# Moving weight means, first shared products and a feed-forward block in a one-core decoder kernel

## The chip, the cores and the metric

The kernel runs on one core of a Trainium2 chip. Five engines work side by side, each with its own in-order queue: TensorE (PE, with PEld for its weight loads), VectorE (DVE), ScalarE (ACT), GpSimd (POOL) and SyncE (SP, which issues the DMAs here). [...] The metric is the time of one execution in microseconds (us) on the device. A profile is one such execution, recorded instruction by instruction; its span runs from the first to the last instruction.

## What is computed

One decoder layer on 16 sequences of 256 tokens with 512 features, in float32:

```python
x = _layernorm(x + mamba(x))            # 2 x + out projection inside
x = _layernorm(x + long_convolution(x, ctx, ctx))
x = _layernorm(x + ffn(x))
```

The first block normalises x, projects it to gate z, inner xi, states B and C and step dt, runs a 4-tap convolution and a state recurrence, and projects back. The second, for each of 32 heads h (8 positions of the 256 each) and along the 512 features:

```python
kv = v[:, :, :, None, :] * x2[:, :, None, :, :]     # 8 x 8 products
y  = irfft(rfft(kv, n) * rfft(k, n), n)[..., :L] + kv * skip
out = einsum('bhijl,bhil->bhjl', y, x1)
```

Here x1 = x2 = ctx. The third is a linear layer with weight W, plus the two best of eight low-rank experts, chosen by a gate.

## The kernel before

**First stage** (to about 757 us): eight groups of 512 tokens. In each, a hand-written list `order` of ten products, counted by i = 0 to 9: ("x", p), ("z", p), ("b", 0), ("c", 1). For each i the program issues `first_products` on TensorE, `finish_products` of the product before, `first_sums` of this one and `finish_sums` of the one before (VectorE and ScalarE). `head_means(0)` and `head_means(1)` (tile `xm`, line 598) come at i = 6 and 8; `yps` at i = 9 (line 679). After the list, `spread_heads` (line 740) spreads a small result over two `mm` banks and two `wh` tiles, and `gated` (line 754) multiplies them into the gates on VectorE. The tiles xm, yps, mw, wh and d_lg take turns in the two PSUM buffers of `ps_t`; a tile waits until the readers of the tile two before it are done.

Three functions prepare the feed-forward weights w_f (128 x 4 x 512) and the gate weights w_gl (128 x 4 x 136), so that the layer norm in front of that block costs nothing later. `with_identity` (line 512) adds the residual to w_f. `chunk_sum` (523) adds the four chunks on GpSimd. `centred` (534) multiplies the sum with a constant matrix on TensorE (tile mw) and subtracts the result from each chunk in four VectorE instructions (540). All three run in group 1: with_identity at i = 2, chunk_sum at i = 3 and 4, centred at i = 5 and 6.

**Second stage** (from about 757 us): 32 heads, each in two parts q = 0 and 1 of eight sequences. The convolution is a product with Toeplitz blocks T. Its result y is four PSUM banks in two pairs: the first holds the output blocks 1 and 0, the second 2 and 3. `convolve` (1018) computes full 128 x 128 blocks (1027) and then quadrants of 64 x 64 (1042). Two products that the blocks 2 and 3 share are formed once: `seeded` (1008) multiplies the Toeplitz block T with xs, a sum on GpSimd (997), into bank 3, and `spread_seed` (1014) copies it by halves on ScalarE, with the halves exchanged, into bank 2 (1016). The convolution adds to both. In the first part of head 0 there is no seed (`late`): the quadrants come first, then six full blocks in the order `FIRST`.

VectorE multiplies each pair of y with the context (`multiplied`, 1077), reduces it (`reduced`, 1087) and prepares the next head's kv (`products`, 156). The new y of the next part takes the same banks, so its first writer into a pair waits for `multiplied` of that pair.

The feed-forward block of head h - 1 runs inside head h: gate products (1190), and four blocks of `feed_forward` (1223) into the tile `base`, for k = 0 to 3, two matmul instructions each. Block 0 stands ahead of the seed of part 1, blocks 1 and 2 behind it, and block 3 at the start of the next head, ahead of `turned_gates` (1213), the seed of part 0 and `lora` (1219). The tile base has one PSUM buffer; heads 0 and the start of head 1 don't use it. `gates` (1115 to 1142) and `store` (1158) go to VectorE and ScalarE.

The order on each engine is that of the program: no scheduler changes it.

Of the kernel before, what the change touches and what calls it, by code (L numbers as in the profile page):

```python
# [8 lines left out]
F32 = mybir.dt.float32  # L9
# [5 lines left out]
P = 128  # L15
B, S, D = 16, 256, 512
# [12 lines left out]
NH = 8  # L29
# [14 lines left out]
SHARED_AT, DIAGONAL_AT = 3, 5  # L44
NT, NC = 6, 6
FIRST = ((1, 0), (2, 0), (2, 1), (3, 0), (3, 1), (3, 2))

QUADRANTS = (
    (0, 0, 1), (1, 0, 1), (2, 0, 1), (3, 0, 1),
# [22 lines left out]
def decoder_kernel(  # L72
# [108 lines left out]
    with ExitStack() as s1:  # L181
# [370 lines left out]
        for g in range(groups):  # L552
# [97 lines left out]
            for i, (kind, p) in enumerate(order):  # L650
                if g == 1 and i == 2:
                    with_identity(w_f)
                if g == 1 and i in (3, 4):
                    w, cols = ((w_f, D), (w_gl, NG))[i - 3]
                    total = chunk_sum(w, cols)
                if g == 1 and i in (5, 6):
                    centred(*sums.pop(0))
                if g == 1 and i in (3, 4):
                    sums.append((w, cols, total))
                if i == 6:  # L660
                    ms = [head_means(0)]
                if g == 0 and i == 0:
                    al, be = first_products(
                        kinds[kind], p, True, None,
                        lambda: begun.append(begin_products(w_xi, order[1][1], False)),
                    )
                else:
                    al, be = first_products(
                        kinds[kind], p, i % 3 == 0, begun.pop(0) if begun else None
                    )  # L670
                if i == 8:
                    ms.append(head_means(1))
                if i == 9:


                    yps = ps_t.tile([P, S], F32, tag="tr", name="yps")
                    for ht in range(HT):
                        for b in range(GB):
                            nc.tensor.matmul(
                                yps[b * HP : (b + 1) * HP],  # L680
                                sel[:, ht].rearrange("p q h -> p (q h)"),
                                Bs[ht][:, b * S : (b + 1) * S],
                                start=(ht == 0),
                                stop=(ht == HT - 1),
                            )
                if before is not None:
                    finish_products()
                to = places(kind, p)
                u = first_sums(al, be, to)
                if i == 8:  # L690
                    states(1, stepped(ms[1], spreads[2]), spreads[3])
                if i == 6:
                    ms = [stepped(ms[0], spreads[0])]
                    spreads.append(spread(1, 1))
                if g == 0:
                    if i == 1:
                        parts = decays()
                    if i == 2:
                        nc.scalar.activation(A, A, AF.Exp)
                        nc.vector.tensor_scalar(A, A, -1.0, None, ALU.mult)  # L700
                    if i in (1, 2, 4):
                        next(parts)
                if i == 9:
                    yT = q3.tile([P, S], F32, tag="vn", name="yT", bufs=1)
                    nc.scalar.copy(yT, yps)
                if before is not None:
                    finish_sums((lambda: next(parts)) if g == 0 and i == 2 else None)
                if g == 0 and i == 3:
                    next(parts)
                if g == 0 and i in later:  # L710
                    for n, (w, k) in enumerate(later[i]):
                        ins = weight_sums(nc.gpsimd, w, k)
                        if n == 0:
                            wait_for(ins, mixes[-1])
                if i == 7:
                    states(0, ms[0], spreads[1])
                if i == 8:
                    outputs(0)
                    outputs(1)
                    if more:  # L720
                        rt = to_dram(rms(xs_next))
                    if g == 0:
                        behind = []
                        w_sums = w_o_sums(behind)
                        next(w_sums)
                before = (kind, p, al, be, u, to)
                if i < 2 and late:
                    normalised(g - 1, late.pop(0))
                if i == 1 and more:
                    xs_next = load_x(g + 1)  # L730
# [186 lines left out]
    with ExitStack() as s2:  # L917
# [87 lines left out]

            return xs, Td, pair_sum, differences

        def seeded(y, T, xs, q):

            nc.tensor.matmul(bank_of(y, 3), T[:, SHARED_AT, :], xs[:, q], start=True, stop=True)  # L1012

        def spread_seed(y):
            for a, b in ((0, HP), (HP, 0)):
                nc.scalar.copy(bank_of(y, 2)[b : b + HP], bank_of(y, 3)[a : a + HP])  # L1016

        def convolve(y, kv, T, Td, q, between=None, late=False, early=None, ahead=None):

            begun = set() if late else {2, 3}

            def full(lb, mb, w):
                nc.tensor.matmul(  # L1027
                    bank_of(y, lb),
                    w,
                    moving(kv, q, mb),  # L1030
                    start=not late and lb not in begun,
                    stop=False,
                    skip_group_check=True,
                )
                begun.add(lb)

            def quadrant(lb, a, b):
                r, c = a ^ (lb in SWAPPED_IN), b ^ (lb in SWAPPED_OUT)
                start = lb not in begun and (lb, c) not in begun
                begun.add((lb, c))  # L1040
                rows, cols = [slice(i * HP, (i + 1) * HP) for i in (r, c)]
                return nc.tensor.matmul(  # L1042
                    bank_of(y, lb)[cols],
                    T[rows, DIAGONAL_AT, (b - a) * HP : (b - a + 1) * HP],
                    moving(kv, q, lb)[rows],
                    start=start,
                    stop=False,
                    skip_group_check=True,
                )

            if not late:
                full(1, 0, T[:, FULL_AT[1, 0], :])
                full(3, 2, T[:, FULL_AT[3, 2], :])
                full(3, 0, Td[:, 1, :])
                full(2, 1, Td[:, 0, :])
            begin = [quadrant(*e) for e in QUADRANTS[:4]]
            one = p2.tile([P, 1], F32, tag="one", name="one")
            seen = nc.scalar.copy(one, nhalf[:, 0:1])
            for ins in begin:
                wait_for(seen, ins)  # L1060
            for e in QUADRANTS[4:8]:
                quadrant(*e)
            for e in QUADRANTS[8:]:
                wait_for(quadrant(*e), seen)
            if late:
                for n, (lb, mb) in enumerate(FIRST):
                    if n == 0 and ahead is not None:
                        ahead()
                    if n == 1 and early is not None:
                        early()  # L1070
                    if n == 3 and between is not None:
                        between()
                    full(lb, mb, T[:, FULL_AT[lb, mb], :])
# [154 lines left out]
        for h in range(HX):  # L1228
# [8 lines left out]
            if h:  # L1237
# [5 lines left out]
                        cTs.append(load_c(h + 2))  # L1243
                if rest is not None:
                    base, o_r, xa = rest
                    feed_forward(base, o_r, (3,))
                    turned = turned_gates(xa)
                seeded(y, T, xs, 0)
                spread_seed(y)
                if rest is not None:  # L1250
                    lora(base, [turned])
            if ff:
# [14 lines left out]
                if ff:  # L1267
                    folded()
            red = p2.tile([P, NQ, NL, BQ * NH], F32, tag="red", name="red")
            convolve(y, kv, T, Td, 0, late=h == 0, ahead=ahead)  # L1270
            if h == 0:
                v_after = vT_ahead[0]
            ws = skip_sum(sk_next)
# [10 lines left out]
            else:  # L1284

                prs = []
                for i in range(2):
                    prs.append(multiplied(y, cT, 0, i))
                    behind = products(v_n, cT_n, kv_n, 0, (i * NL // 2,), kept)
                for i, pr in enumerate(prs):  # L1290
                    reduced(pr, red, 0, i)
            y = new_y()

# [8 lines left out]
                base = ps_b.tile([P, D], F32, tag="base", name="base")  # L1302
                feed_forward(base, o_l, (0,), True)
            if nxt:
                seeded(y, T, xs, 1)
            if ff:
                feed_forward(base, o_l, (1, 2) if nxt else (1, 2, 3))
            if ready is not None:
                store(*ready)
            if nxt:  # L1310
                spread_seed(y)
            if nxt:
                products(v_n, cT_n, kv_n, 1)
                more_next = prepared(kv_n, T_n)
# [168 lines left out]
```

## Time and profile before

| what | value |
| --- | --- |
| median of 3 runs | 1433.55 us (1432.08 to 1434.61) |
| the profiled execution | 1433.9 us |
| its span | 1432.1 us |
| TensorE busy | 1414.5 us |
| VectorE busy | 1210.5 us |
| GpSimd busy | 492.3 us |
| ScalarE busy | 414.5 us |
| mean granted TensorE clock | 0.997 |

In lists of waits each line names who waited, for whom, the total in us, how often and the longest. A line of a timeline has the start, the length in us, the engine, the line of the kernel, the operation, output and inputs, the shape and how many instructions were merged; in brackets the idle time of the engine before it and who ended it. A float32 matmul shows as two instructions. Neighbouring TensorE instructions overlap in the record[...]: 512 columns start 0.43 us apart and last 0.59. A granted clock of 1.0 is TensorE's full speed.

### The profile page before, as it was taken

The page shows a single profiled execution, that of the slowest core. Times are in us where ns is not written, and L with a number is a line of the kernel's source. Part 1 is how long each engine was busy: PE and PEld are TensorE (multiplying, and loading weights), DVE is VectorE, ACT ScalarE, POOL GpSimd, SP SyncE. Part 2 cuts the span into 40 slices and gives each one's busy share as a digit, 9 for nine tenths or more (in the row PEclk, how much of TensorE's full clock was granted, in tenths as well). Part 3 has the DMA queues.
Part 4 walks back from the last instruction along what each step waited for, and adds up shares of the span by engine and source line. Part 5 has one row for each costly group of instructions (what it writes and reads, how often), then busy time and mean ns, then how long its engine had stood idle before and what let it go on. Part 6 is the DMA issues. An engine that isn't in the chain of part 4 may idle for free.

```text
span 1432.1 us, 18826 instructions
## 1 busy us (share of the span) xinstructions
PE 1414.5 (99%) x6882; PEld 908.0 (63%) x6882; DVE 1210.5 (85%) x2133; ACT 414.5 (29%) x900; POOL 492.3 (34%) x662
## 2 busy tenths in 40 slices
PE   9999999999999999999999999999999999999997
PEld 7887788787888888888884444444444444444443
DVE  6978778877888787887847999999999999999996
ACT  3423323233232332322301323222322232222221
POOL 5451010100100201002005565556555655565562
PEclk9999999999999999999999999999999999999999
DMA  8013021120121201212002212221222122112200
GB/s 299 33 39 130 14 76 46 38 83 8 58 68 40 79 13 39 83 44 84 15 26 96 66 45 73 67 73 45 75 66 65 54 74 67 60 59 67 73 26 23
DMA packets 49165, 89.16 MB, mean 62 GB/s; under 512 B 8880, under 2 KB 13360, under 8 KB 49072
## 3 DMA queue, kind: packets, MB, share of 16 engines
q1 hardware_dynamic: 49072, 87.96, 19.2%
q8 instruction: 54, 0.88, 0.3%
q14 instruction: 39, 0.32, 0.1%
HBM read 70.62 MB, written 17.32 MB: 61 GB/s over the span
## 4 chain that ended last, share of the span: by engine, by line
PE 87%; DVE 2%; issue 1%; POOL 1%; ACT 0%; POOLq 0%; DVEq 0%
PE mm L329 16%; PE y L1027 15%; PE y L1042 12%; PE s L329 11%; PE base L1223 8%; PE s L783 5%; PE mm L783 5%; PE y L1012 4%; PE gl L1190 2%; PE base L1219 2%; PE tr L146 1%; PE xm L598 1%; PE mm L740 1%; PE mm L874 1%; PE s L874 1%
## 5 line engine op out<-in xcount | busy, mean ns | idle before, releaser
L1077 DVE TENSOR_TENSOR pr<-y,cT 128x1024 f32<-128x1024 f32 x126 | 148.1, 1217 | 47.1 <-PE y L1042 47.1
L1042 PE MATMUL y<-kv 64*64 64x512 f32 x1536 | 179.6, 598 | 0.0
L587 DVE SCALAR_TENSOR_TENSOR acc<-xi,wc,acc 128x512 f32<-128x512 f32 x192 | 141.9, 753 | 7.4 <-ACT acc L583 1.7
L1087 DVE TENSOR_REDUCE red<-pr 128x128 f32<-128x1024 f32 x126 | 147.1, 1208 | 0.0
L156 DVE TENSOR_TENSOR kv<-tr,cT 128x1024 f32<-128x1024 f32 x124 | 145.4, 1213 | 0.0
L1027 PE MATMUL y<-kv 128*128 128x512 f32 x272 | 128.2, 594 | 0.6 <-ACT y L1016 0.4
L1042 PEld LDWEIGHTS y<-kv 64*64 64x64 f32 x1536 | 52.2, 132 | 119.0 <-issue 96.7
L1223 PE MATMUL base<-w_f,ol 128*128 128x512 f32 x248 | 124.0, 603 | 0.0
L1027 PE MATMUL y<-kv,Td 128*128 128x512 f32 x248 | 116.5, 592 | 0.0
L67 POOL TENSOR_TENSOR rs_a<-ve_a,nhalf 128x1 f32<-128x1 f32 x32 | 19.0, 594 | 243.0 <-DVE ve_a L65 243.0
L1256 POOL TENSOR_TENSOR ol<-o,red 128x512 f32<-128x512 f32 x31 | 39.4, 1271 | 181.3 <-DVE red L1087 181.3
L390 POOL TENSOR_TENSOR rstd<-ms,nhalf 128x4 f32<-128x4 f32 (+1 forms) x9 | 8.5, 949 | 255.4 <-DVE ms L388 255.4
L1027 PEld LDWEIGHTS y<-kv 128*128 128x128 f32 x272 | 51.1, 190 | 66.4 <-issue 48.9
L329 PE MATMUL mm<-XT,w_z 128*128 128x256 f32 x384 | 90.7, 379 | 0.0
L1016 ACT COPY y<-y 64x512 f32<-64x512 f32 x124 | 69.2, 558 | 64.4 <-PE y L1012 62.4
L1027 PEld LDWEIGHTS y<-kv,Td 128*128 128x128 f32 x248 | 47.1, 190 | 59.3 <-issue 59.3
L997 POOL TENSOR_TENSOR xs<-kv 128x512 f32<-128x512 f32 x63 | 80.2, 1274 | 0.1
L329 PEld LDWEIGHTS mm<-XT,w_z 128*128 128x128 f32 x384 | 73.0, 190 | 9.9
L329 PE MATMUL mm<-xnT,w_z 128*128 128x256 f32 x288 | 71.0, 382 | 0.0
L1012 PE MATMUL y<-xs,kv 128*128 128x512 f32 x124 | 65.7, 611 | 2.8 <-DVE pr L1077 1.6
L329 PE MATMUL s<-XT,w_xi 128*128 128x256 f32 x256 | 61.0, 380 | 1.2 <-DVE XT L222 0.7
L1223 PEld LDWEIGHTS base<-w_f,ol 128*128 128x128 f32 x248 | 42.4, 191 | 30.9 <-issue 30.9
(279 smaller groups left out, 2810.1 us busy)
## 6 DMA issues: line engine op xcount, KB each, us to landing
cT<-in_ctxT SPq DMA_DIRECT2D x32, 384.0 KB
kv<-in_toep SPq DMA_DIRECT2D x32, 384.0 KB
xt<-in_x SPq DMA_DIRECT2D x32, 256.0 KB
spread<-both SPq DMA_DIRECT2D x32, 256.0 KB
first<-xt SPq DMA_DIRECT2D x32, 256.0 KB
vn<-first SPq DMA_DIRECT2D x32, 256.0 KB
out<-res SPq DMA_DIRECT2D x31, 256.0 KB
xnT<-in_xT SPq DMA_DIRECT2D x7, 1024.0 KB
```

Of the source, the lines that this page charges most:

```text
L156: last = nc.vector.tensor_tensor(kv[:, q, k * BQ : (k + NL // 2) * BQ], vT[:, q, blks].rearrange("p k (b i) -> p (k b) i", i=NH).unsqueeze ...
L329: nc.tensor.matmul(ps, w[:, p, a, kc, :], Xs[b][:, kc, :], start=start and kc == 0, stop=stop and kc == 1, skip_group_check=upon,)
L587: ins = nc.vector.scalar_tensor_tensor(acc, xi[:, :, k : k + S], wc[:, c, k : k + 1], acc, ALU.mult, ALU.add)
L783: nc.tensor.matmul(ps, own[a][c][:, n * P : (n + 1) * P], w_o[b][c], start=start and c == 0, stop=stop and c == HC - 1, skip_group_check=upon,
L997: return nc.gpsimd.tensor_tensor(xs[:, q], moving(kv, q, 0), moving(kv, q, 1), ALU.add)
L1012: nc.tensor.matmul(bank_of(y, 3), T[:, SHARED_AT, :], xs[:, q], start=True, stop=True)
L1016: nc.scalar.copy(bank_of(y, 2)[b : b + HP], bank_of(y, 3)[a : a + HP])
L1027: nc.tensor.matmul(bank_of(y, lb), w, moving(kv, q, mb), start=not late and lb not in begun, stop=False, skip_group_check=True,)
L1042: return nc.tensor.matmul(bank_of(y, lb)[cols], T[rows, DIAGONAL_AT, (b - a) * HP : (b - a + 1) * HP], moving(kv, q, lb)[rows], start=star ...
L1077: nc.vector.tensor_tensor(pr.rearrange("p (k b j) i -> p k b j i", k=2, j=NH), y[i].rearrange("p k (b j i) -> p k b j i", j=NH, i=NH), cT[ ...
L1087: nc.vector.tensor_reduce(red[:, q, 2 * i : 2 * i + 2, :].rearrange("p k t -> p (k t)"), pr, AX.X, ALU.add)
L1223: nc.tensor.matmul(base, o_l[:, kc, :], w_f[:, kc, :], start=(first and kc == kcs[0]), stop=False)
```

## The change

Four edits, none of which changes a result:

1. `chunk_sum` and `centred` leave group 1. In group 2 the sum of w_f, in group 3 that of w_gl is formed at i = 5 on GpSimd; the product and the subtractions are issued at i = 9 of the same group, behind yps and ahead of `finish_products`. with_identity stays in group 1.
2. The first part of head 0 does its full blocks in the order AHEAD, with block (1, 0) last. VectorE then takes one `products`, the second pair of y, the first pair, and the other `products`; before, it took first pair, products, second pair, products.
3. The seeds of head 0, part 1 and of head 1, part 0 are formed in the base bank (tag base) instead of y's bank 3. ScalarE copies them into bank 3, a whole bank, and then by halves into bank 2.
4. Block 2 of `feed_forward` goes from behind the seed of part 1 to the start of the next head, beside block 3.

```diff
+AHEAD = ((2, 0), (2, 1), (3, 0), (3, 1), (3, 2), (1, 0))
...
-                if g == 1 and i in (3, 4):
-                    w, cols = ((w_f, D), (w_gl, NG))[i - 3]
-                    total = chunk_sum(w, cols)
-                if g == 1 and i in (5, 6):
-                    centred(*sums.pop(0))
-                if g == 1 and i in (3, 4):
-                    sums.append((w, cols, total))
+                if g in (2, 3) and i == 5:
+                    w, cols = ((w_f, D), (w_gl, NG))[g - 2]
+                    sums.append((w, cols, chunk_sum(w, cols)))
...
                                 start=(ht == 0),
                                 stop=(ht == HT - 1),
                             )
+                    if sums:
+                        centred(*sums.pop(0))
                 if before is not None:
                     finish_products()
...
-        def seeded(y, T, xs, q):
-            nc.tensor.matmul(bank_of(y, 3), T[:, SHARED_AT, :], xs[:, q], start=True, stop=True)
+        def seeded(y, T, xs, q, apart=False):
+            seed = bank_of(y, 3)
+            if apart:
+                seed = ps_b.tile([P, BQ * NH * NH], F32, tag="base", name="yc")
+            nc.tensor.matmul(seed, T[:, SHARED_AT, :], xs[:, q], start=True, stop=True)
+            return seed
-        def spread_seed(y):
+        def spread_seed(y, seed, apart=False):
+            if apart:
+                nc.scalar.copy(bank_of(y, 3), seed)
             for a, b in ((0, HP), (HP, 0)):
-                nc.scalar.copy(bank_of(y, 2)[b : b + HP], bank_of(y, 3)[a : a + HP])
+                nc.scalar.copy(bank_of(y, 2)[b : b + HP], seed[a : a + HP])
...
-                for n, (lb, mb) in enumerate(FIRST):
+                for n, (lb, mb) in enumerate(FIRST if ahead is None else AHEAD):
...
-                    feed_forward(base, o_r, (3,))
+                    feed_forward(base, o_r, (2, 3))
                     turned = turned_gates(xa)
-                seeded(y, T, xs, 0)
-                spread_seed(y)
+                seed = seeded(y, T, xs, 0, h == 1)
+                spread_seed(y, seed, h == 1)
...
-            convolve(y, kv, T, Td, 0, late=h == 0, ahead=ahead)
+            convolve(y, kv, T, Td, 0, late=h == 0, ahead=None if h else ahead)
...
-                for i in range(2):
-                    prs.append(multiplied(y, cT, 0, i))
-                    behind = products(v_n, cT_n, kv_n, 0, (i * NL // 2,), kept)
-                for i, pr in enumerate(prs):
+                products(v_n, cT_n, kv_n, 0, (0,), kept)
+                prs = [multiplied(y, cT, 0, i) for i in (1, 0)]
+                behind = products(v_n, cT_n, kv_n, 0, (NL // 2,), kept)
+                for i, pr in zip((1, 0), prs):
                     reduced(pr, red, 0, i)
...
-                seeded(y, T, xs, 1)
+                seed = seeded(y, T, xs, 1, h == 0)
             if ff:
-                feed_forward(base, o_l, (1, 2) if nxt else (1, 2, 3))
+                feed_forward(base, o_l, (1,) if nxt else (1, 2, 3))
...
-                spread_seed(y)
+                spread_seed(y, seed, h == 0)
```

## The prediction

> **What bounds the kernel now.** First the page's busy row and the waits of TensorE:
>
> ```profile
> PE 1414.5 (99%) x6882; PEld 908.0 (63%) x6882; DVE 1210.5 (85%) x2133; ACT 414.5 (29%) x900; POOL 492.3 (34%) x662
> ...
> PE xm L598 <- DVE w_f L540: 3.0, 1, 3.0
> ...
> PE y L1012 <- DVE pr L1077: 1.6, 1, 1.6
> PE xat L1213 <- DVE xa L1135: 0.9, 1, 0.9
> PE y L1012 <- POOL xs L997: 0.8, 1, 0.8
> ...
> PE y L1027 <- ACT y L1016: 0.4, 1, 0.4
> ```
>
> TensorE stands still for only 17.6 us of 1432.1. The change leaves the number of its multiplications as it is, so it can win only stalls. The list names three that it touches: 3.0 us (the weight means in group one), 1.6 and 0.4 us (second part of head 0), 0.8 us (start of head 1). The timeline says what the 3.0 us really cost:
>
> ```profile
> 140.03 0.40 PE L537 MATMUL mw<-g_sum,share 128*128 128x136 f32 x2
> 143.46 1.83 PE L598 MATMUL xm<-acc,mean 128*32 128x512 f32 x8 [3.03 <-DVE w_f L540]
> 145.22 2.01 PE L329 MATMUL s<-xnT,w_bc 128*128 128x256 f32 x4
> ...
> 237.06 1.06 PE L598 MATMUL xm<-acc,mean 128*32 128x512 f32 x8
> 238.06 1.13 PE L329 MATMUL s<-xnT,w_bc 128*128 128x256 f32 x4
> ```
>
> The same two rows take 2.89 us in group one (the second of the code's groups from zero) and 2.19 in group two; after the stall everything crawls. The windows view gives a granted clock of 0.54 from 143.4 to 147.1 us, the only slow stretch in the first stage. The start of the second head means (L598) in the groups 0 to 3 is 63.82, 161.83, 253.79 and 345.75: distances 98.01, 91.96, 91.96. So group one costs 6.05 us more than its neighbours.
>
> The start of the second stage, TensorE, then VectorE:
>
> ```profile
> 768.01 1.10 PE L1012 MATMUL y<-xs,kv 128*128 128x512 f32 x2 [1.64 <-DVE pr L1077]
> 768.95 1.02 PE L1027 MATMUL y<-kv 128*128 128x512 f32 x2
> 770.40 1.13 PE L1027 MATMUL y<-kv 128*128 128x512 f32 x2 [0.43 <-ACT y L1016]
> ...
> 777.34 1.10 PE L1012 MATMUL y<-xs,kv 128*128 128x512 f32 x2 [0.77 <-POOL xs L997]
> ```
> ```profile
> 764.40 1.21 DVE L1077 TENSOR_TENSOR pr<-y,cT 128x1024 f32<-128x1024 f32 x1
> 765.53 1.21 DVE L156 TENSOR_TENSOR kv<-tr,cT 128x1024 f32<-128x1024 f32 x1
> 766.66 1.21 DVE L1077 TENSOR_TENSOR pr<-y,cT 128x1024 f32<-128x1024 f32 x1
> ```
>
> The seed at 768.01 follows the multiplication that ends at 766.66 + 1.21 = 767.87: it needs the pair y1, which that instruction reads.
>
> A steady head, TensorE, VectorE and ScalarE:
>
> ```profile
> 920.43 1.02 PE L1223 MATMUL base<-w_f,ol 128*128 128x512 f32 x2
> 921.29 0.27 PE L1213 MATMUL xat<-ident,xa 128*128 128x128 f32 x1
> 921.54 1.10 PE L1012 MATMUL y<-xs,kv 128*128 128x512 f32 x2
> 922.48 1.02 PE L1219 MATMUL base<-w_lb,xaT 128*128 128x512 f32 x2
> ```
> ```profile
> 920.23 2.35 DVE L1077 TENSOR_TENSOR pr<-y,cT 128x1024 f32<-128x1024 f32 x2
> ```
> ```profile
> 922.68 1.15 ACT L1016 COPY y<-y 64x512 f32<-64x512 f32 x2 [0.81 <-PE y L1012]
> ```
>
> Here TensorE has no gap, yet the seed at 921.54 comes just after VectorE's first multiplication ends (920.23 + about 1.22 = 921.45). So a head of 20.6 us is a tie of two paths: TensorE's queue, and VectorE from the first part's multiplication (929.70) through products and gates to the second part's (940.86), which frees the bank of the next seed.
>
> **What the Trainium skill says.** "TensorE: Matmul & The Clock Gate", section "What's actually happening", says that about 3.4 us without work halves the clock for a window of the same order. The trace agrees: 3.03 us idle, then 0.54; the 1.64 us at 768 are followed by matmuls at the usual 0.43 us spacing. "SBUF — State Buffer", section "Who interferes with whom", says that a VectorE tensor_scalar from SBUF can hold a port pair shared with GpSimd, and that whoever comes second waits. The trace agrees: L546 takes 0.55 us at 220.47, but 1.69 at 762.19, where a GpSimd product starts at 762.12.
>
> **The change, part by part** (TensorE time; minus is gain).
>
> *Weight means, group one emptied.* Of the 6.05 us two waits of about 0.1 us each at 124 to 126 remain: there TensorE waits for first_sums, held up by with_identity, which stays (that row is 2.11 us for eight, 1.89 in group two). The rest goes: two products for w_f (0.86), two for w_gl (about 0.3), the stall, and the half clock. -5.8.
>
> *Group two, w_f.* Added: the mw product, 2 x 0.43 = +0.86, between yps and finish_products. GpSimd's three additions (1.27 each) fall at 220.4 to 224.3, where GpSimd is idle from 220.44 to 259.96; but they start beside L546 (220.47), as at 762.12, and hold it up by about 1 us. with_identity delays the same place by 0.9 us in group one and costs TensorE 0.22; I take +0.3, bounds 0 and 0.6. Then VectorE: today its first_sums of the last product start at 260.68. Now the four subtractions come first, on an in-order queue. They begin when mw ends, 262.05 + 0.43 + 0.59 = 263.1, and take 2.47 us (group one: 2.47 for four), to 265.6. After them: first_sums (1.3), last_sums (0.65), then gated, four steps of 0.6 us, ending at 269.9 instead of 268.48. TensorE wants the last wh bank for spread_heads(1) at 268.71 + 0.86 = 269.58: stall +0.4, bounds 0 and 1.2. The mw bank itself is free at 265.6, when spread_heads(0) wants it at 265.7: nothing. Later uses of VectorE's sums have two us of slack (S1 ends at 274.4, used at 276.78). Sum +1.6.
>
> *Group three, w_gl.* Product +0.3; four subtractions of 0.29 us end at 263.4 in group two's clock, before VectorE must wait for finish_products anyway (264.94): nothing more. GpSimd's additions are 0.43 us each. +0.3.
>
> First stage: -5.8 + 1.6 + 0.3 = -3.9.
>
> *Head 0.* The order AHEAD completes banks 2 and 3 (y1) after five blocks, at 765.5, and (1,0) at 766.4. VectorE: product 764.40, y1 765.56, y0 766.69 to 767.91, product to 769.0: as many instructions as before. The seed goes to the free base bank, so it starts at 766.2 instead of 768.01 and ends at 767.2. ScalarE now copies three times: a full bank (0.59, as the vT copy L148) at 767.3 to 767.9, then two halves to 769.0. full(1,0) needs y0: 768.0; full(3,2) needs only the first copy: 768.94 instead of 770.40. With the first-matmul delays, the transposes start at 774.35 instead of 775.91: -1.56.
>
> *Head 1.* The seed need not wait for y1. It waits for xs of part 0 (GpSimd, done at 773.95, tied to a VectorE product that stays at 769.0) and for the transposes: start 774.86. VectorE's multiplications move to 774.46 and 775.6, ending at 776.8; then full(1,0) at 776.9, full(3,2) at 777.84. Before, full(3,2) followed the half copies, which ended at 779.62, and began at 779.68. Gain at this point 1.84, and with the slow first pair after that wait 1.94. What is late next: y0 on VectorE.
>
> *feed_forward (2, 3).* One block of 0.86 us moves in thirty heads from behind the seed of part 1 to the next head's start. Both places lie on TensorE's path between the same two points of the tie (end of quadrants 0, next seed), so it moves nothing by itself: 0. It takes away cover: full(3,2) of part 1 had 1.23 us between ScalarE's copy and itself, now 0.37. That is exactly part 0's pattern (seed, one block, full(1,0), full(3,2), copies ending at 923.83, full(3,2) at 924.20), which runs without a gap. The store (res, 931.03 to 931.84) still lies before the copies (932.78). Bounds: -0.05 and +0.4 us a head.
>
> *Last head.* Its seed waits 0.37 us for VectorE; the moved block was ahead of it already: 0.
>
> Sum: -3.9 - 1.9 = -5.8 us. The profiled execution took 1433.9 us around its span of 1432.1, 0.35 above the median of 1433.55; I subtract from the median: 1427.8.
>
> **The rivals.**
> 1. *Only the first stage pays*: the seed of head 1 waits for GpSimd's xs of part 1, as the list of waits has it (POOL xs L997). For it: that name, ending at 777.30. Against: VectorE's y1 ends at 777.24, which explains the start as well, and the seed reads part 0. Then the second stage gives 0.6 and the whole is 1429.0.
> 2. *Group two costs as much as group one did*: VectorE's delay grows through port conflicts or the banks to a stall near 3 us, with the half clock again (1.6). +3 to +4 on my sum, 1431.5. For it: four slow instructions ahead of sums that TensorE waits for. Against: 0.4 us by the count.
> 3. *Slower*: full(3,2) of part 1 waits for ScalarE in each steady head. The slack is 0.37 us to the matmul, about 0.13 to its weight load. If the store or anything else holds the copies up by another whole copy (0.56 us), the stall is 0.4 us, less the tie's 0.1: 30 x 0.3 = +9, giving 1436.8. It decides from 0.2 us a head on (30 x 0.2 = 6 cancels the gain). For it: thin cover, thirty times. Against: part 0 does the same today.
>
> **How the numbers follow.** The measurement tells 0.2%, 2.9 us, from no change. My forecast 0.64 (1426.3 to 1429), rival 1 0.16, rival 2 0.12, rival 3 0.08. Faster than 1430.7: all of the first two cases, 0.80, and 0.02 of rival 2: 0.82. Within 0.2%: 0.10 of rival 2 and a weak form of rival 3, 0.12 together. Slower: 0.06. The range takes in the bounds of group two, rival 1 and part of rival 2: 1425.5 to 1431.
>
> **What would show it.** Right: no wait of xm for w_f and no clock of 0.5 in the first stage; distances between L598's starts of about 92.2 (group one), with 1.6 more in group two and 0.3 in group three; wh (L740) stalled once by some 0.4 us on L754; seeds at about 766.2 and 774.9 less the 3.9; a steady head still 20.6 us, with full(3,2) of part 1 right behind full(1,0). Wrong: a head longer than 20.7 us with an idle time in front of L1027 from the seed's copies, a second clock dip, or the head-1 seed starting only when xs of part 1 is done.

## The result, and the profile after

| | before | after |
| --- | --- | --- |
| median | 1434.0 us (1432.08 to 1435.12, 7 runs) | 1428.76 us (1428.54 to 1429.45, 7 runs) |
| profiled execution | 1433.9 us | 1429.05 us |
| its span | 1432.1 us | 1427.3 us |

The ratio of the times is 0.9964, with an interval of 0.9953 to 0.9976: 5.2 us faster. The forecast was 1427.8, the range 1425.5 to 1431.

The busy row of the page of the changed kernel, and then its list of waits (who waited for whom; total, times, longest, in us):

```profile
PE 1413.3 (99%) x6882; PEld 906.7 (64%) x6882; DVE 1211.9 (85%) x2133; ACT 415.2 (29%) x902; POOL 492.4 (34%) x662
```
```profile
PE y L1030 <- DVE pr L1080: 1.7, 2, 1.0
```

TensorE has as many instructions as before, and ScalarE two more, the full copies. From the list of waits the 3.0 us of xm for w_f are gone, and so are the waits of the seeds for VectorE and GpSimd and that of a full block for ScalarE. Among the places that the change touches, the line shown is new: two waits for `multiplied`. They are what is late next in the heads 0 and 1; for head 1 the prediction said so ("What is late next: y0 on VectorE", y0 being the first pair of y). At the very start, before anything that the change touches, TensorE waits 0.6 us for the first weights' DMA; this execution is 0.26 us behind the one of before there.

The starts of the second head means in the groups 0 to 3 (timeline of TensorE, tile xm):

```profile
64.08 1.06 PE L599 MATMUL xm<-acc,mean 128*32 128x512 f32 x8
156.26 1.07 PE L599 MATMUL xm<-acc,mean 128*32 128x512 f32 x8
248.50 1.07 PE L599 MATMUL xm<-acc,mean 128*32 128x512 f32 x8
341.77 1.06 PE L599 MATMUL xm<-acc,mean 128*32 128x512 f32 x8
```

The distances are 92.18, 92.24 and 93.27, where 98.01, 91.96 and 91.96 stood, and the next one is 92.20 (91.96). Group 1 is 5.83 us shorter. Part of that is the clock: the same stretch of group 1 in the timeline of TensorE, and in the windows view (length; busy time and count of PE, PEld, DVE, ACT, POOL; granted clock; DMA share; GB/s):

```profile
139.53 1.06 PE L599 MATMUL xm<-acc,mean 128*32 128x512 f32 x8
140.53 1.13 PE L330 MATMUL s<-xnT,w_bc 128*128 128x256 f32 x4
```
```profile
138.00:142.00 4.00, 4.00 (x23) 2.54 (x22) 3.77 (x7) 1.56 (x3) 0.00 (x0) 1.00 0.00 0
```

No idle time, a clock of 1.00, and the two rows take 2.13 us from the start of the first to the end of the second, in place of 3.77 (143.46 to 147.23 in the trace of before).

Now the place that got the work, group 2. VectorE, then TensorE:

```profile
214.91 1.48 DVE L547 TENSOR_SCALAR xt<-xt,mv_a,rs_a 128x512 f32<-128x512 f32 x1 [0.73 <-POOL rs_a L68]
```
```profile
264.29 0.48 PE L739 MATMUL mm<-yT,w_h 32*128 32x256 f32 x2
...
265.79 1.56 PE L782 MATMUL s<-w_o,zs 128*128 128x256 f32 x6
```

L547 takes 1.48 us beside GpSimd's first addition (214.84 to 216.11), not 0.55. The four subtractions run from 257.91 to 260.39 on VectorE, ahead of `first_sums`. And TensorE needs 1.50 us from the start of the second `spread_heads` (264.29) to the product behind it (265.79); before, the same two rows started at 268.70 and 269.77, 1.07 apart. The difference, 0.43, is the forecast stall for wh. No list of waits shows it: it falls between matmuls whose recorded ends run over it. All in all group 2 costs 0.28 us more at its start and 1.31 at its end, the product's 0.86 included.

The start of the second stage, TensorE and then ScalarE:

```profile
764.22 2.28 PE L1030 MATMUL y<-kv 128*128 128x512 f32 x4 [0.73 <-DVE pr L1080]
...
773.40 1.98 PE L1030 MATMUL y<-kv 128*128 128x512 f32 x4 [1.00 <-DVE pr L1080]
```
```profile
764.17 1.15 ACT L1019 COPY y<-yc 64x512 f32<-64x512 f32 x2
```

The seeds start at 762.47 and 771.38. The rows at 764.22 and 773.40 are the same four instructions, full(1,0) and full(3,2): the full blocks from input block 0 into output block 1 and from 2 into 3. The first row lasts 2.28 us, the second 1.98. Single instructions show why: at head 0, full(3,2) starts at 765.37, just behind ScalarE's last half copy (the full one ran from 763.57 to 764.14; 764.17 + 1.15 = 765.32). At head 1 the copies end before full(3,2) would start anyway.

Measured from start to start, against the trace of before: the first stage is 4.00 us shorter, head 0 is 1.29 shorter, head 1 0.39. From there the heads run alike, 20.63 to 20.64 us in both, but for one head of which more is said below. Here is the place where block 2 went, and further down the place that it left, in a steady head of the changed kernel; TensorE, then ScalarE:

```profile
914.17 1.88 PE L1226 MATMUL base<-w_f,ol 128*128 128x512 f32 x4
915.89 0.27 PE L1216 MATMUL xat<-ident,xa 128*128 128x128 f32 x1
916.15 1.10 PE L1012 MATMUL y<-xs,kv 128*128 128x512 f32 x2
...
927.19 1.02 PE L1226 MATMUL base<-w_f,ol 128*128 128x512 f32 x2
928.05 1.88 PE L1030 MATMUL y<-kv 128*128 128x512 f32 x4
```
```profile
927.39 1.15 ACT L1019 COPY y<-y 64x512 f32<-64x512 f32 x2 [0.94 <-PE y L1012]
```

Four base instructions (blocks 2 and 3, from 914.17) now stand ahead of xat (915.89) and the seed of part 0 (916.15). Behind the seed of part 1 (926.33) stands only one block, then full(1,0) and full(3,2) without a gap: ScalarE is done at 928.54, and full(3,2) is due at 928.05 + 0.86 = 928.91. Only its weight load (PEld) already waits 0.35 us for the copies, until 928.59, and that costs nothing here.

### The profile page after: what moved, and what is told of

Same layout as the page of the kernel before. It is cut to its first block, busy times and chain, and to the rows that moved or that the text cites. A ratio compares the mean times of both kernels' runs of the same rounds, so it can differ in the third digit from the quotient of the medians.

```text
span 1427.3 us, 18820 instructions
## 1 busy us (share of the span) xinstructions
PE 1413.3 (99%) x6882; PEld 906.7 (64%) x6882; DVE 1211.9 (85%) x2133; ACT 415.2 (29%) x902; POOL 492.4 (34%) x662
## 4 chain that ended last, share of the span: by engine, by line
PE 97%; DVE 1%; issue 1%; DMA 0%; SPq 0%; POOL 0%; POOLq 0%; ACT 0%; DVEq 0%
PE mm L330 21%; PE y L1030 15%; PE s L330 14%; PE y L1045 12%; PE base L1226 8%; PE s L782 6%; PE mm L782 6%; PE y L1012 4%; PE gl L1193 2%; PE base L1222 2%; PE tr L147 1%; PE xm L599 1%; PE mm L739 1%; PE mm L873 1%; PE s L873 1%
```

## Experiments

The times are medians, and each ratio is to runs of the kernel before on the same chip; differences between two runs of the table are rougher. Shifts "in the trace" are differences of starts between two profiled executions.

| run | what | median us (runs) | ratio to before, interval |
| --- | --- | --- | --- |
| means | edit 1 alone | 1430.22 (12) | 0.9974, 0.9966 to 0.9983 |
| seeds | edits 2 and 3 | 1432.51 (13) | 0.9991, 0.9983 to 1.0000 |
| block | edit 4 alone | 1434.27 (13) | 1.0004, 0.9996 to 1.0012 |
| order | edit 2 alone | 1432.79 (12) | 0.9995, 0.9987 to 1.0004 |
| apart | edit 3 alone | 1432.75 (12) | 0.9992, 0.9984 to 1.0001 |
| bare | after, no block behind the seed | 1440.50 (2) | 1.0050, 1.0032 to 1.0068 |
| one_group | both means in group 1, late | 1430.14 (9) | 0.9976, 0.9967 to 0.9986 |
| mended | after, group 2 set right | 1428.02 (5) | 0.9961, 0.9949 to 0.9974 |
| late_halves | after, half copies later | 1435.40 (10) | 1.0016, 1.0007 to 1.0025 |
| unlocked | mended, GpSimd behind the gates | 1420.46 (4) | 0.9911, 0.9897 to 0.9924 |
| old_unlocked | before, GpSimd behind the gates | 1428.78 (5) | 0.9965, 0.9952 to 0.9977 |

### The parts of the change, alone

Edit 1 alone (means):

```diff
-                if g == 1 and i in (3, 4):
...
+                if g in (2, 3) and i == 5:
...
+                    if sums:
+                        centred(*sums.pop(0))
```

> Before plus the first edit alone (weight means in groups 2 and 3). My theory: group 1 gives back 5.8 us (stall of xm, half clock, two products), group 2 pays 1.6 (0.3 for the GpSimd additions beside L546, 0.9 for the mw product, 0.4 for wh), group 3 pays 0.3: -3.9 us, ratio about 0.9973, and from head 0 on a constant shift. Rival (the edits help only together, or the stall merely moves to group 2): 0 to -1.5 us. The distances of the second head means in groups 0 to 4 should be 92.2, 92.2, 93.3, 92.2.

Measured: distances 92.20, 92.24, 93.28 and 92.20, the same as in the changed kernel, and 3.9 us less in the medians. So the first stage gains the same with and without the other edits.

Edits 2 and 3 (seeds), and edit 4 (block):

```diff
+AHEAD = ((2, 0), (2, 1), (3, 0), (3, 1), (3, 2), (1, 0))
...
+                seed = seeded(y, T, xs, 0, h == 1)
+                spread_seed(y, seed, h == 1)
```

> Before plus the second and third edit (order in head 0, seeds in the base bank). My theory: only the start of heads 0 and 1 changes, by -1.3 us in head 0 and -0.4 in head 1, then a constant shift: -1.7 us, ratio about 0.9988. Rival (the shift is eaten by the tie of VectorE and TensorE in the heads after): 0 us, with a shift that shrinks from head to head.

```diff
-                    feed_forward(base, o_r, (3,))
+                    feed_forward(base, o_r, (2, 3))
...
-                feed_forward(base, o_l, (1, 2) if nxt else (1, 2, 3))
+                feed_forward(base, o_l, (1,) if nxt else (1, 2, 3))
```

> Before plus the fourth edit alone (block 2 at the start of the next head). My theory: 0 us (within 0.3), a steady head stays 20.63 us, quadrants of part 1 begin 0.86 us earlier in the head and nothing else moves. Rival (the moved block gives the seed of part 0 cover from VectorE): -0.1 us a head, -3 us. Rival (thinner cover for the seed's copies): +0.2 us a head or more, +6 us.

Measured: the seeds give 1.29 us in head 0 and 0.39 in head 1, and the shift stays to the end. The block gives nothing: the head is 20.63 to 20.64 us, although the quadrants of part 1 begin 0.86 us earlier in it; over 30 heads the trace drifts by 0.24 us the other way.

The medians of seeds and before differ by 1.6 us, which is what the two heads give. Its profiled execution lies only 0.4 us below that of before (1433.53 and 1433.9), because its group 1 was 99.19 us long, 1.2 more than in the trace of before. The windows view of that run:

```profile
139.00:143.00 4.00, 1.54 (x9) 1.18 (x7) 3.93 (x7) 1.17 (x3) 0.00 (x0) 0.95 0.00 0
143.00:147.00 4.00, 3.44 (x12) 1.50 (x13) 3.17 (x10) 0.96 (x2) 0.00 (x0) 0.50 0.00 0
147.00:151.00 4.00, 4.00 (x15) 3.26 (x14) 0.32 (x1) 0.37 (x1) 0.00 (x0) 0.70 0.00 0
```

While the clock is low it is 0.5, so the shares 0.95, 0.50 and 0.70 make 6.8 us of half clock. In the trace of before the same three windows have 1.00, 0.58 and 1.00: 3.4 us. The six traces in which the stall stands know these two lengths only: 3.4 us in before, block, order and apart, with a group 1 of 97.81 to 98.02 us, and 6.8 us in seeds and old_unlocked, with 99.19 and 99.27. The length goes with the moment at which the clock falls, which no run sets on purpose: in the two it falls 0.97 and 0.81 us before the stall ends; in apart 0.38 us before, and in the other three 0.16 to 0.50 us after. The work that runs at half clock takes twice its time, so half of the low stretch outside the stall is lost: by this estimate 1.7 us in before and 2.9 in seeds, and 1.2 is the difference of the two groups.

"TensorE: Matmul & The Clock Gate", section "What's actually happening", in the Trainium skill says that the window is free-running, so that the point of change depends on where in it the work falls. The two lengths agree with that. Its figure of about 3.4 us without work, which the prediction uses, does not hold as a limit here: stalls of 3.02 to 3.04 us lowered the clock in six traces of six, while in the trace of late_halves (below) TensorE stands still for 3.54 us and the windows view has a clock of 1.00 from 777.0 to 780.5 us. So the length of a stall alone doesn't decide.

Which of the two edits earns what (order, then apart):

```diff
-                for n, (lb, mb) in enumerate(FIRST):
+                for n, (lb, mb) in enumerate(FIRST if ahead is None else AHEAD):
...
-                    prs.append(multiplied(y, cT, 0, i))
...
+                prs = [multiplied(y, cT, 0, i) for i in (1, 0)]
...
```

> Before plus the second edit alone (order in head 0, seed still in bank 3). My theory: the seed of part 1 waits for the second pair until 766.85 instead of 768.01 (old clock), its copies end at 769.1, full(3,2) follows at 769.2 instead of 770.40: -1.2 us in head 0, 0 in head 1; with the base bank's -1.0 this is more than the -1.7 of both, since both shorten the same wait. Rival (the order only helps with the base bank): 0.

```diff
+            if apart:
+                seed = ps_b.tile([P, BQ * NH * NH], F32, tag="base", name="yc")
...
```

> Before plus the third edit alone (seeds of head 0 part 1 and head 1 part 0 in the base bank, old order in head 0). My theory: in head 0 the seed starts 1.8 us earlier, but the three copies wait for VectorE's second multiplication (767.87 in the old clock) and end at 769.65, and full(3,2) follows the last of them: -0.7 us there, -0.4 in head 1, so -1.1 us of the -1.7 that both edits give; the order is worth the other 0.6. Rival (the base bank does all of it): -1.7 us.

Measured in the traces: order 1.09 us in head 0 and nothing in head 1; apart 0.63 and 0.39. Both intervals of the times include 1, so only the traces speak here. In head 0 the two overlap: 1.09 + 0.63 is 1.72, together they give 1.29. In head 1 the base bank alone gives the gain.

### How thin the cover is in a steady head

The prediction's slower rival had ScalarE's copies late for full(3,2) of part 1. This run takes the last block away too, so the copies must be late:

```diff
-                    feed_forward(base, o_r, (2, 3))
+                    feed_forward(base, o_r, (1, 2, 3))
...
-                feed_forward(base, o_l, (1,) if nxt else (1, 2, 3))
+                feed_forward(base, o_l, () if nxt else (1, 2, 3))
```

> The changed kernel with block 1 moved as well: (1, 2, 3) at the start of the next head and none behind the seed of part 1. My theory: the copies of the seed end 1.78 us after its second matmul starts, and full(3,2) would start after 1.29, so it waits about 0.55 to 0.65 us in each of 29 heads, of which the tie hides 0.1: a head of 21.1 us, +13 to +17 us on the whole. Rival (TensorE's order in part 1 doesn't matter because VectorE sets the length of a head): 0 to +3 us.

Full(3,2) of part 1 in its timeline of TensorE:

```profile
910.11 1.12 PE L1030 MATMUL y<-kv 128*128 128x512 f32 x2 [0.38 <-ACT y L1019]
```

ScalarE's copies run from 908.91 to 910.06, and full(3,2) starts at 910.11, 1.40 us behind full(1,0) (908.71) instead of 0.86: 0.54, and its pair takes 1.12 in place of 1.02. Of these 0.64 us a head loses 0.42 (21.05 us against 20.63), since the next seed no longer waits for VectorE: it follows xat by 0.11 us (918.69, 918.80) instead of 0.26, and its pair takes 1.02 instead of 1.10. The kernel is 11.7 us slower than the changed one. So the rival's mechanism is real; the one block left behind the seed keeps it away. The tie hid 0.22 us a head, where the prediction and the expectation had put about 0.1, and the cost came out below the expected 13 to 17 us for that reason.

### Does the group matter, or the place in the list?

Both means stay in group 1, but are issued as late as edit 1 issues them (from the kernel before):

```diff
+                if g == 1 and i == 5:
+                    for w, cols in ((w_f, D), (w_gl, NG)):
+                        sums.append((w, cols, chunk_sum(w, cols)))
...
+                    while sums:
+                        centred(*sums.pop(0))
```

> Before with both weight means still in group 1, but with the additions at i = 5 and products and subtractions of both at i = 9. My theory: the place in the list matters and not the group: 2.3 us are paid (1.3 for w_f as in the changed kernel, 0.3 for the second product, 0.7 more wait of wh), 5.8 saved: -3.5 us against before, no half clock. Rival (group 1 is the crowded one): the stall comes back with the half clock, 0 to -1.5 us.

Measured: 92.18, then 94.11, a net gain of 3.68 us in the trace, against 4.0 for edit 1; the times (ratios 0.9976 and 0.9974) can't tell the two apart. So nearly all of the gain comes from the place at the end of the list, not from the other groups. The added wait was of another kind than expected: in the trace the product of w_gl stands behind 0.55 us of idle time that ScalarE's yT ends.

### What group two still costs

Mended leaves the product where edit 1 puts it, but issues the four subtractions behind `first_sums`, and lets GpSimd's first addition wait for the layer norm's last VectorE instruction (L547 before, L551 here):

```diff
+            wait_for(ins, scaled[-1])
...
-                        centred(*sums.pop(0))
+                        means.append(centred(*sums.pop(0)))
...
+                while means:
+                    subtracted(*means.pop())
```

> The changed kernel with two mends: the four subtractions stand behind first_sums of i = 9, and GpSimd's first addition waits for the layer norm's last VectorE instruction (L547). My theory: group 2 loses its 0.28 us at the start (L547 back at 0.55 us) and 0.35 us at wh, so the distances of the second head means are 92.2, 92.0, 92.9, 92.2: -0.6 us against the changed kernel, ratio to before 0.9959. Rival (the cost of group 2 is the product and its place in TensorE's queue alone): no difference from the changed kernel.

VectorE, then TensorE, in group 2 of this run:

```profile
214.55 0.55 DVE L551 TENSOR_SCALAR xt<-xt,mv_a,rs_a 128x512 f32<-128x512 f32 x1 [0.72 <-POOL rs_a L68]
```
```profile
263.66 0.48 PE L746 MATMUL mm<-yT,w_h 32*128 32x256 f32 x2
...
264.74 1.56 PE L789 MATMUL s<-w_o,zs 128*128 128x256 f32 x6
```

L551 is back at 0.55 us, the two rows of TensorE are 1.08 us apart again, and the distances are 92.19, 91.96, 92.85 and 92.19: what remains of group 2 is the product itself, 0.89. The median is 0.7 us below the changed kernel's, but the intervals of the two ratios overlap widely, so here too the traces speak and not the times. So the two small terms that the prediction had for L546 and wh were the right ones.

### Is it the first copy or the last that full(3,2) waits for?

In head 0 the gain was 0.27 us short. If full(3,2) waits for the half copies, although they go into the other bank of its pair, then issuing them behind it should free it:

```diff
+            def halves():
+                for a, b in ((0, HP), (HP, 0)):
+                    nc.scalar.copy(bank_of(y, 2)[b : b + HP], seed[a : a + HP])
...
+                if halves is not None:
+                    halves()
```

> The changed kernel, with the two half copies of the first two base-bank seeds issued behind full(3,2) instead of ahead of it. Theory A (the wait of full(3,2) is for its own bank alone; the prediction's step): it starts right behind full(1,0), the halves run as before: -0.3 us in head 0, 0 in head 1. Theory B (waits between engines are kept by pair of banks): full(3,2) starts early, but the halves wait for it and the next block for them: +1.1 us in head 0 and +1.3 us in head 1, +2.4 us in all.

TensorE, then ScalarE, in the heads 0 and 1:

```profile
764.57 1.98 PE L1034 MATMUL y<-kv 128*128 128x512 f32 x4 [0.73 <-DVE pr L1086]
767.88 1.95 PE L1034 MATMUL y<-kv,Td 128*128 128x512 f32 x4 [1.33 <-ACT y L1018]
...
780.54 1.95 PE L1034 MATMUL y<-kv,Td 128*128 128x512 f32 x4 [3.54 <-ACT y L1018]
```
```profile
766.59 1.15 ACT L1018 COPY y<-yc 64x512 f32<-64x512 f32 x2 [2.10 <-PE y L1034]
...
778.59 0.63 ACT L1187 ACTIVATE sq<-ol 128x512 f32<-128x512 f32 x1 [3.96 <-POOL ol L1265]
```

It was the last: with only the full copy ahead of it, the pair of blocks takes 1.98 us, no longer 2.28. But the halves then wait for full(3,2), which writes the other bank, and the next block waits for the halves: 1.33 us of idle time. In this program the waits are between pairs of banks, not banks, in both directions. In head 1 the halves are also queued behind an activation that waits for GpSimd until 778.59 (they run from 779.24 on), and TensorE stands for 3.54 us. Against the changed kernel head 0 loses 1.27 us in the trace, near theory B's 1.1, and head 1 3.77, where theory B had 1.3 because it left that queue out. The whole is slower than the kernel before. The median lies 6.6 us above the changed kernel's, more than the 5.0 of the two heads. The mean granted clock of its ten executions goes from 0.998 in the two fastest (the profiled one is among them) to 0.996 in the two slowest; that the long stall lowers the clock in some of them fits this, but no trace of a slow one was kept.

### What sets the head

Moving 0.86 us changed nothing, because the next seed waits for VectorE in both kernels. In the changed one the seed at 916.15, shown above, follows the first multiplication of this row (914.84 + about 1.22 = 916.06):

```profile
914.84 2.35 DVE L1080 TENSOR_TENSOR pr<-y,cT 128x1024 f32<-128x1024 f32 x2
```

Why is VectorE so late? In the gates of the kernel before two tiny comparisons stand out (VectorE, then GpSimd):

```profile
936.88 0.21 DVE L1124 TENSOR_TENSOR cmp<-lg 128x64 f32<-128x64 f32 x1
937.01 1.50 DVE L1125 TENSOR_TENSOR cmp<-lg 128x64 f32<-128x64 f32 x1
938.44 1.31 DVE L1126 TENSOR_TENSOR cmp<-cmp,tri 128x64 f32<-128x64 f32 x1
```
```profile
936.95 1.49 POOL L933 TENSOR_TENSOR sk<-kv,skip_bc 128x512 f32<-128x512 f32 x1
938.39 1.28 POOL L997 TENSOR_TENSOR xs<-kv 128x512 f32<-128x512 f32 x1
```

The first row, L1124, has the same 64 columns as the two behind it and takes 0.21 us. Each of the long ones begins just behind the start of a GpSimd product and ends just behind its end. "SBUF — State Buffer", section "Who interferes with whom", in the Trainium skill says that a VectorE instruction with two inputs from SBUF contends with a GpSimd instruction that reads SBUF, and that the loser is blocked, not slowed; these numbers agree. To test it, the two GpSimd products are put behind the comparisons: unlocked on top of mended, old_unlocked on the kernel before.

```diff
+            if behind is not None:
+                wait_for(ins, behind)
...
-                sk_next = skip_sums(h + 1, kv_n)
+            compared = None
+            if ff:
+                xa, compared = gates(gl, rs)
+            if nxt:
+                sk_next = skip_sums(h + 1, kv_n, compared)
                 more_next[2](1)
-            if ff:
-                xa = gates(gl, rs)
...
```

> The mended kernel, with GpSimd's skip products (sk) and the second xs issued behind the gates, the first of them waiting for the gate comparison, so that VectorE's two comparisons no longer run beside GpSimd (today 1.5 and 1.3 us, alone 0.2). My theory: VectorE's half of the tie becomes about 2.4 us shorter, the seed of part 0 no longer waits, and TensorE's own queue sets the head: 20.63 becomes 20.48 us, -0.15 us a head as the bare kernel showed, -4.5 us on top of the mended kernel, and no more. Rival (no tie, TensorE alone sets the head): 0. Rival (VectorE alone sets it): up to -2.4 us a head, -70 us.

> The kernel before with only the GpSimd products moved behind the gates, as in the unlocked kernel. My theory: the tie was there before the change and the change did not touch it, so a head goes from 20.63 to 20.41 us here too: 31 x 0.22 = 6.8 us, with the end of the last head 7 to 7.5 us, ratio about 0.995. Rival (the fourth edit made the room for it): 0 to -3 us.

Unlocked, the timeline of VectorE:

```profile
909.33 0.22 DVE L1138 TENSOR_TENSOR cmp<-cmp,tri 128x64 f32<-128x64 f32 x1
...
909.99 1.16 DVE L1142 SCALAR_TENSOR_TENSOR ex<-rank,ex 128x8 f32<-128x8 f32 x1
...
911.99 2.36 DVE L1089 TENSOR_TENSOR pr<-y,cT 128x1024 f32<-128x1024 f32 x2 [0.25 <-PE y L1054]
```

Both comparisons take 0.22 us. VectorE now waits 0.25 us for TensorE's quadrants, the next seed follows xat by 0.11 us (914.10, 914.21), and its pair takes 1.02 instead of 1.10. The head is 20.41 us; the kernel takes 1420.46 us, 13.3 below the kernel before and 8.3 below the changed one. It is the fastest kernel of this study. Against mended it gains 7.6 us, where 4.5 was expected: 0.22 us a head and not 0.15, the same 0.22 that bare had shown the tie to hide. One lock has moved, not gone: L1142 now takes 1.16 us, not 0.17, beside sk (909.63 to 911.12).

Old_unlocked, VectorE:

```profile
920.21 2.36 DVE L1079 TENSOR_TENSOR pr<-y,cT 128x1024 f32<-128x1024 f32 x2 [1.12 <-PE y L1044]
```

The head is 20.45 us, 0.18 less than in the kernel before. VectorE waits 1.12 us for the quadrants, against 0.25 in unlocked: the 0.86 that edit 4 brings forward. Only with the lock gone does this early start pay, and then 0.04 us a head: the seed's pair still takes 1.06 us here and 1.02 in unlocked. The expectation, 20.41 us a head and 6.8 us, was missed: the heads give 5.5 us in the trace and the medians differ by 4.9. Its rival, 0 to -3 us, was missed too.

## Why the prediction was right

By its own steps:

- **Group one emptied**: -5.8 forecast, -5.83 measured. The stall and its half clock were one item, and both went. One reading on the way was wrong: the two rows that the prediction puts at 2.89 us take 3.77 by the lines that it shows; no later step uses the number. "The trace agrees" said too much of the clock, too: 3.03 us of idle time is less than the figure of about 3.4 us beside it. And the close match has luck in it: the 98.01 us came from one execution, and in two of six traces with the stall the group was 1.2 us longer.
- **Group two and three**: +1.6 and +0.3 forecast; +0.28 + 1.31 = +1.59, and +0.24. First stage -3.9, measured -4.00. Mended showed that the small terms are the ones named.
- **Head 1**: -0.38, measured -0.39. The seed did not wait for xs of part 1, so rival 1 fell there; y0 on VectorE is late next, 1.00 us.
- **Head 0**: -1.56, measured -1.29. This is the step that failed: "full(3,2) needs only the first copy: 768.94". It waited for the last half copy, which goes into the other bank of the pair. The term was 0.27 us too large; late_halves showed the cause.
- **Block 2 moved**: 0 forecast. The head kept its 20.63 us. "Exactly part 0's pattern" held, with 0.37 us of cover between copies and full(3,2), and rival 3 did not come about; bare showed what it would have cost, 0.42 us a head. "Less the tie's 0.1" was mis-sized: the tie hides 0.22.
- **Rival 2**, a new stall of 3 us in group two, fell: there is no half clock in the traces of after, means or one_group in the first stage.

The sum of the stages is 0.26 (the start, not the change's) - 4.00 - 1.29 - 0.39 = -5.42 behind head 1. At the end of the heads it is -4.98, and in the spans -4.8. Most of the 0.44 up to the end of the heads comes from one head of 20.92 us, in which one comparison takes 0.48 us instead of 0.21; the same head is long in means and late_halves, and in no other trace. In the changed kernel's trace that comparison (L1127, 1137.85 to 1138.33) ends just behind a GpSimd product (L1001, 1137.51 to 1138.24), which came 0.3 us later than in the other heads, so it looks like the same lock as in the section above. Why GpSimd was late there stays open, as does the rest, below 0.01 us a head. Against the profiled execution's own time the sum, 5.8, was 0.95 us too large (1433.9 - 1429.05 = 4.85): 0.27 from head 0, 0.26 from the start, 0.44 from these heads, small items the rest.

## What to carry to other kernels

A stall of TensorE costs more than its length where the clock falls with it, here by about 1.5 to 3 us on top of 3.0, by the same estimate as above; look at the granted clock of each execution, and measure the distance between equal points of equal loop passes, not the stall. Before moving work to make an engine's input earlier, ask whether the consumer is itself late for another reason: here 0.86 us a head were worth nothing until VectorE was freed from GpSimd. And look for tiny instructions with long durations: a neighbour of equal shape shows what they take alone, and an engine whose instruction ends with them is the first suspect; moving that instruction tests it.

## What was not expected of the hardware

- Two GpSimd products of 1.49 and 1.28 us stretched two VectorE instructions of 64 columns from 0.22 to 1.50 and 1.31 us and so held each head about 0.2 us above what TensorE's own queue needs; reordering them gave 0.18 us a head in the kernel before and 0.22 in the mended one. No list of waits shows this, because the blocked time counts as busy: VectorE's busy time falls from 1210.5 us in before to 1171.9 in old_unlocked, with 2133 instructions in both.
- After a stall of 3.0 us the low clock lasts 3.4 or 6.8 us in these traces, nothing between: group 1 took 97.81 to 98.02 us in the four traces with the one, 99.19 and 99.27 in the two with the other, and 92.18 to 92.20 in the traces without the stall. A stall of 3.54 us in another place left the clock at 1.00. The times of the kernel before follow the clock: of 79 executions beside the experiments, those with a mean granted clock of 0.998 took 1431.8 to 1433.5 us, those with 0.996 1434.7 to 1436.1. They spread over 3.0 us in the result and the changed kernel's over 0.9. A kernel with the stall need not spread so far, though: the twelve runs of order lie within 1.0 us.
- In these traces a matmul that has just been released costs a little more than the gap shows: its pair takes 1.10 to 1.12 us instead of 1.02, and a seed that waits for VectorE without showing idle time starts 0.26 us behind its predecessor instead of 0.11.
